# A post-norm decoder layer on one core: the next batch's first queries, keys and score maxima computed inside this batch's self attention, and cross attention scores issued for four heads at a time

## The chip, the cores and the metric

The program runs on one core of one Trainium2 chip. The metric is the device time in microseconds (us) of one execution; lower is better. TensorE is called PE here, VectorE DVE, ScalarE ACT, GpSimd POOL and SyncE SP, as the profile calls them.

## The reference

Four batches of 1024 tokens of width 256 pass through one decoder layer in float32: self attention, cross attention and a mixture of experts, each followed by a residual and a layer norm.

```python
# self attention: 16 heads of 16, scores scaled by a gate per token and head
q, k, v = heads(x @ Wq + bq), heads(x @ Wk + bk), heads(x @ Wv + bv)
scores = q @ k.T / 4 * sigmoid(x @ cg_W + cg_b + (cons_vec @ am_W + am_b))
ctx = softmax(scores) @ v
ctx = 0.3 * ctx + 0.7 * mha(x, ca)          # 4 heads of 64
ctx = (1 - META_W) * ctx + META_W * mha(ctx, mc)
x = layernorm(x + ctx @ Wo + bo)
# cross attention: 16 heads of 16, 154 keys, bias -log(distance) * |scaling|
scores = (x @ WqT + bq) / 4 @ (ctx1024 @ WkT + bk).T + bias
x = layernorm(x + softmax(scores) @ (ctx1024 @ WvT + bv) @ WoT + bo)
# top 2 of 8 experts per token, and a shared expert
x = layernorm(x + experts(x) + shared(x))
```

## The kernel before, in words

**Layout.** Token tiles have 128 partitions; `xT`, `cm` and `x1T` hold a batch transposed (features on partitions, 1024 tokens along the row). The 16 narrow heads sit four to a group of 128 partitions, each in its own 32 rows (`r = 32 * j`), so a matmul of one head uses 32 rows of PE's array. PSUM, where matmuls write, is split into a `big` ring of two tiles of two banks, a `small` ring of three tiles of one bank (`one` in the profile), and one `acc` tile.

**Self attention of a batch** (lines 944 to 979) is a loop of 128 steps. A step has two halves, for two pairs of heads that use different rows:

- `maxima(n + 12)`, lines 473 to 497: the scores of two heads, queries on partitions and 512 keys along the row (two matmuls into a `big` tile, L485), and DVE's maximum over them (L492). After every eight steps the maxima are transposed and written as one more row of the queries, so that the second scores come out with the maximum already taken off.
- `exponentials(n)`, lines 499 to 561: the scores again, keys on partitions (four matmuls of 256 columns, L518), ACT's exponential (L529), and, three steps later and once in two steps, the product with the values (L539) into a `small` tile.

The maxima run `lead = 12` steps ahead. In the last 12 steps of a batch there are none left, and `exponentials` is called with `alone=True`: its scores go into one `big` tile and one exponential of 1024 columns reads them (L526).

**Where the lead comes from.** `begin(b)` (lines 832 to 854) prepares a batch: two transposes of the tokens into `xT`; for each half of the heads a gate, the queries and the keys (`project`, three times 8 matmul instructions at L344), which go out to DRAM (`q_rows`, `k_rows`) and come back with padding rows (`load`); then 12 calls of `maxima`, each followed by one of the 8 value projections `wv` (L358), and 8 value projections for the 4-head attention. Batch 0 runs this at once. For later batches it is the generator `ahead`, advanced step by step in the batch before: twice beside the output projection (L1010 to 1014), eight times in `close_sublayer` (L1022 to 1024), and then once in each step of the cross loop.

**The rest of a batch.** Four query and key projections of the `ca` attention (`caq`) and its first two units run in the last 12 to 28 steps of self attention. Then come the `ca` and `mc` attentions (L593, L629, L647; 16 units each), the output projection, a layer norm, the keys and values of cross attention, and the cross loop (lines 1104 to 1115, 36 turns).

**The cross loop.** `scores(n)` (L717 to 752) handles two heads and two token tiles: four matmuls of 154 keys into one `big` tile (L725), then for each of the four blocks DVE adds the bias and takes the minimum (`biased`, recorded at L325) and ACT takes the exponential (L745). `flip(n - 2)` transposes (L760) into a `small` tile that ACT copies (L763), and at odd turns the last 32 keys of all four heads (L770) into another that DVE copies (L777). `product` (L786, L795) multiplies with the values into `acc`, ACT copies it (L803), and `divide` (L407 to L411) normalizes.

**What sets the order.** The source gives each engine's instructions an order; the builder's scheduler may then move a ready instruction ahead. It also assigns ring slots, so an instruction that writes a tile waits for the ring's slot to come free. The `ex` ring of SBUF tiles (10 slots, `EXB`) carries exponentials, gates, outgoing queries and keys, and transposed probabilities; the `qk` ring has 6 slots.

Of the kernel before, what the change touches and what calls it, by code (L numbers as in the profile page):

```python
# [1 line left out]

# [14 lines left out]
P = 128  # L17
# [7 lines left out]
EXB = 10  # L25
# [17 lines left out]
def run(gen):  # L43
    for _ in gen:
        pass
# [3 lines left out]
def decoder_layer(ctx: ExitStack, tc: tile.TileContext, a, out):  # L49
# [11 lines left out]
    def big():  # L61
        return pbig.tile([P, 2, 512], F32, tag="big", name="big")
# [145 lines left out]
    with tc.tile_pool(name="wA", bufs=1) as wA, tc.tile_pool(name="work", bufs=2) as work:  # L208
# [90 lines left out]
        bv = load_bcast("bv", a["L0_attn_bv"])  # L299
        for i in range(2):  # L300
            for half in range(NC2):
                nc.sync.dma_start(rows_of(i, half, HD), pads[:, i, :])

        def load_mha(k, w_out):
            win = wide.tile([P, NC2, 3 * H], F32, tag=k, name=k + "win")
            nc.sync.dma_start(win, a[f"L0_attn_{k}_Win"].rearrange("(c p) n -> p c n", p=P))
            bin_ = a[f"L0_attn_{k}_bin"]
            mbq = load_cols(k + "bq", bin_[0:H])
            mbk = load_cols(k + "bk", bin_[H : 2 * H])
            mbv = load_bcast(k + "bv", bin_[2 * H : 3 * H])  # L310
            wout = load_plain(k + "wout", a[f"L0_attn_{k}_Wout"], H)
            bout = load_cols(k + "bout", a[f"L0_attn_{k}_bout"])
            nc.vector.tensor_scalar(bout, bout, w_out, None, ALU.mult)
            return win, mbq, mbk, mbv, wout, bout
# [21 lines left out]
        def qk_tile(name):  # L336
            return work.tile([P, S], F32, tag="qk", name=name, bufs=6)
# [365 lines left out]
        class Cross:  # L703
# [13 lines left out]
            def scores(self, n):  # L717
                g, s = divmod(n, 8)
                tp, pair = divmod(s, 2)
                ps = big()  # L720
                for tt in range(2):
                    for jj in range(2):
                        r = 32 * (2 * pair + jj)
                        tok = (2 * tp + tt) * P
                        nc.tensor.matmul(  # L725
                            ps[:, jj, tt * S2 : (tt + 1) * S2],
                            self.q[g][r : r + 32, tok : tok + P],
                            self.kx[r : r + 32, g, :],
                            start=True,
                            stop=True,  # L730
                        )
                ex = ex_tile([P, 2, 2, S2], "xs")
                mx = work.tile([P, 4], F32, tag="xmx", name="xmx", bufs=3)
                for tt in range(2):
                    for jj in range(2):
                        biased(
                            ex[:, jj, tt, :],
                            ps[:, jj, tt * S2 : (tt + 1) * S2],
                            self.bias[:, 2 * tp + tt, :],
                            mx[:, 2 * tt + jj : 2 * tt + jj + 1],  # L740
                        )
                for tt in range(2):
                    for jj in range(2):
# [8 lines left out]
                self.ex[n] = ex  # L752
# [79 lines left out]
        def begin(b):  # L832

            y = ys[b]
            xT = work.tile([P, NC2, S], F32, tag="xT", name="xT", bufs=1)
            for c in range(NC2):
                transpose_tokens(xT, y, c)
                yield
            v16 = work.tile([P, NT, VP], F32, tag="v16", name="v16", bufs=1)
            nc.gpsimd.memset(v16, 1.0)  # L840
            sa = Self(xT, v16, None)
            yield from sa.project(0)
            sa.load(0)
            yield from sa.project(1)
            add_bias(y, bo)
            v64 = work.tile([P, NT, H], F32, tag="v64", name="v64", bufs=1)
            begun[b] = sa, xT, v64
            vals = values(xT, wv, 0, bv, v16, NH, HD, 1)
            for n in range(lead):
                sa.maxima(n)  # L850
                next(vals, None)
                sa.clock.step()
                yield
            yield from values(xT, ca[0], 2 * H, ca[3], v64, MH, MD, 0)
# [58 lines left out]
        run(begin(0))  # L913
# [15 lines left out]
        nds = wA.tile([P, 1], F32, tag="nds", name="nds")  # L929
        nc.sync.dma_start(nds, a["ds"].to_broadcast([P, 1]))  # L930
        nds2 = work.tile([P, 1], F32, tag="nds2", name="nds2", bufs=1)
        nc.vector.tensor_scalar(nds2, nds, -1.0, None, ALU.mult)
        nc.vector.tensor_tensor(nds, nds, nds2, ALU.min)

        behind = iter(())
        for b in range(B):
# [7 lines left out]
            sa, xT, v64 = begun[b]  # L944
# [4 lines left out]
            units = None  # L949
            for n in range(total):  # L950
# [3 lines left out]
                sa.exponentials(n, n + lead >= total)  # L954
# [55 lines left out]
            ahead = begin(b + 1) if b + 1 < B else shared_early(b - 1)  # L1010
# [85 lines left out]
            nc.vector.tensor_scalar(bf, bf, nds, None, ALU.mult)  # L1096
# [7 lines left out]
            for n in range(total + 4):  # L1104
                if n < total:
                    xa.scores(n)
                    if n % 8 == 3 and n // 8 < NG - 1:
                        xa.project_q(n // 8 + 1)
# [392 lines left out]
```

## Time and profile before

| what | us |
|---|---|
| median of 3 runs (lowest, highest) | 3205.32 (3201.66, 3207.2) |
| the profiled execution, and its span | 3203.9, 3202.1 |
| busy in the span: PE, DVE, ACT, POOL | 3100.6, 1652.9, 1613.0, 455.2 |
| batch 0 up to its first self attention step | 0 to 89.5 |
| self attention of batch 0, steps with maxima; steps without | 89.5 to about 288; to about 324 |
| `ca` and `mc` attentions | 324 to 538 |
| output projection, norm, preparation of the cross loop | 538 to 592 |
| cross loop of batch 0 | 592 to about 700 |
| first self attention steps of batches 1, 2, 3 | 702.2, 1333.5, 1965.8 |
| experts | about 2605 to 3202 |

The table's stretches are read from the timeline by the lines that run in them. Matmuls are float32 and each is recorded as two instructions, which is why L485 counts 2048 instructions for 1024 matmuls. Matmuls on different rows of the array overlap in the records, so the time that one costs is taken from the start of its group to the start of the next, not from its own duration.

### The profile page before, as it was taken

What the parts mean: (1) busy time and instruction counts of PE and PEld (TensorE: products, weight loads), DVE (VectorE), ACT (ScalarE), POOL (GpSimd) and SP (SyncE); (2) the same over time, 40 slices, a digit from 0 to 9 for tenths busy, and PEclk for the clock granted to TensorE, in tenths of its full rate; (3) what the DMA queues carried; (4) which work ended last, traced back from release to release, by engine and by line L of the source; (5) the groups of instructions that cost most, each with busy time, mean ns of one, the idle gap of its engine ahead of it and who ended that gap; (6) DMA issues with size and microseconds to landing.
All of it is one profiled execution on the core that took longest, in us unless ns stands there. A gap on an engine that the chain in (4) does not pass through costs nothing.

```text
span 3202.1 us, 61771 instructions
## 1 busy us (share of the span) xinstructions
PE 3100.6 (97%) x25602; PEld 1956.8 (61%) x25602; DVE 1652.9 (52%) x3459; ACT 1613.0 (50%) x3235; POOL 455.2 (14%) x757
## 2 busy tenths in 40 slices
PE   7999999999999999999999999999999999899995
PEld 3665766566657665666576666665666665566663
DVE  3774655567746555677465565774555551111112
ACT  1676534466756344667554346766453631233333
POOL 1111001001110000011100100110000016333331
PEclk7999999999999999999999999999999999999997
DMA  7300000101000001100000100000000052222224
GB/s 222 101 2 1 1 1 2 49 29 41 2 1 1 1 17 37 38 28 2 1 1 1 34 23 23 15 2 11 1 11 1 5 203 104 66 45 47 47 45 125
DMA packets 83325, 111.04 MB, mean 35 GB/s; under 512 B 8832, under 2 KB 69224, under 8 KB 83048
## 3 DMA queue, kind: packets, MB, share of 16 engines
q1 hardware_dynamic: 69752, 89.33, 9.0%
q0 software_dynamic: 13296, 17.77, 3.3%
q8 instruction: 204, 3.34, 0.4%
q14 instruction: 73, 0.60, 0.1%
HBM read 58.97 MB, written 48.11 MB: 33 GB/s over the span
## 4 chain that ended last, share of the span: by engine, by line
PE 89%; DMA 4%; ACT 2%; DVE 2%; issue 1%; POOL 1%; SPq 0%; ACTq 0%; POOLq 0%; DVEq 0%
PE big L485 9%; PE one L539 8%; PE big L593 8%; PE one L629 8%; PE big L1334 8%; PE big L344 8%; PE acc L647 8%; PE one L518 7%; PE acc L1360 4%; PE one L358 3%; PE big L725 3%; PE one L760 2%; PE big L693 2%; DMA scratch<-y,where 1%; PE big L518 1%
## 5 line engine op out<-in xcount | busy, mean ns | idle before, releaser
L492 DVE TENSOR_REDUCE mxp<-big 128x2 f32<-128x1024 f32 x512 | 611.4, 1220 | 239.2 <-PE one L518 169.2
L485 PE MATMUL big<-k,q 31*128 31x512 f32 x2048 | 562.0, 630 | 9.7 <-DMA k<-k_rows 3.7
L529 ACT ACTIVATE ex<-one 128x512 f32<-128x512 f32 x696 | 372.9, 597 | 255.3 <-PE one L518 189.1
L518 PE MATMUL one<-q,k 32*128 32x256 f32 x2784 | 479.1, 397 | 0.0
L325 DVE CUSTOM_DVE_ANT_0 prob<-big,zero_t 128x1024 f32<-128x1024 f32 x256 | 303.8, 1222 | 272.3 <-PE big L593 272.1
L518 PEld LDWEIGHTS one<-q,k 32*128 32x128 f32 x2784 | 322.1, 185 | 27.7 <-DVE q L402 9.2
L612 ACT ACTIVATE prob<-prob,nmx 128x1024 f32<-128x1024 f32 x256 | 293.0, 1152 | 18.6 <-DVE nmx L325 18.5
L634 ACT COPY pt<-one 128x512 f32<-128x512 f32 x256 | 137.7, 590 | 302.7 <-PE one L629 302.7
L539 PE MATMUL one<-ex,v 128*32 128x256 f32 x4096 | 278.4, 390 | 1.5
L593 PE MATMUL big<-mk,mq 64*128 64x512 f32 x1024 | 278.4, 616 | 0.0
L629 PEld LDWEIGHTS one<-ident,prob 128*128 128x128 f32 x2048 | 219.0, 140 | 96.3 <-issue 90.1
L485 PEld LDWEIGHTS big<-k,q 31*128 31x128 f32 x2048 | 195.2, 188 | 129.2 <-issue 102.4
L1334 PE MATMUL big<-wall,xt 128*128 x568 | 268.3, 596 | 1.9 <-issue 1.9
L555 POOL TENSOR_TENSOR avq<-avq,avp 128x256 f32<-128x256 f32 x192 | 139.2, 725 | 887.4 <-ACT avp L554 887.4
L629 PE MATMUL one<-ident,prob 128*128 128x128 f32 x2048 | 255.2, 277 | 0.1
L518 PE MATMUL acc<-q,k 32*128 32x256 f32 x928 | 247.3, 385 | 0.0
L1344 DVE TENSOR_TENSOR hidr<-big,slr 128x512 f32<-128x512 f32 x71 | 49.1, 691 | 373.5 <-ACT slr L1342 373.5
L745 ACT ACTIVATE xs<-xs,xmx 128x154 f32<-128x154 f32 x512 | 175.2, 412 | 109.7 <-DVE xmx L325 109.7
L539 PEld LDWEIGHTS one<-ex,v 128*32 128x32 f32 x4096 | 107.7, 110 | 147.6 <-ACT ex L529 80.6
L636 DVE COPY pt<-one 128x512 f32<-128x512 f32 x256 | 164.3, 683 | 9.1 <-PE one L629 9.1
L518 PEld LDWEIGHTS acc<-q,k 32*128 32x128 f32 x928 | 163.8, 184 | 0.0
L325 DVE CUSTOM_DVE_ANT_0 xs<-big,bias 128x154 f32<-128x154 f32 x512 | 132.6, 313 | 53.4 <-PE big L725 45.6
(270 smaller groups left out, 4590.3 us busy)
## 6 DMA issues: line engine op xcount, KB each, us to landing
scratch<-empty SPq DMA_DIRECT2D x1, 9159.0 KB
xg<-scratch SPq DMA_DIRECT2D x71, 129.0 KB
q<-q_rows SPq DMA_DIRECT2D x16, 512.0 KB
k<-k_rows SPq DMA_DIRECT2D x16, 512.0 KB
y<-in_x_dram SPq DMA_DIRECT2D x4, 1024.0 KB
q_rows<-qh SPq DMA_DIRECT2D x8, 512.0 KB
k_rows<-kh SPq DMA_DIRECT2D x8, 512.0 KB
wall<-in_L_ffn_w_gate_dram SPq DMA_DIRECT2D x8, 512.0 KB
```

Of the source, the lines that this page charges most:

```text
L325: nc.vector.tensor_tensor_reduce(out=out, in0=ps, in1=bias, scale=-1.0, scalar=3.0e38, op0=ALU.add, op1=ALU.min, accum_out=low,)
L344: nc.tensor.matmul(ps[:, tb, :], w[:, c, lo : lo + P], xT[:, c, tb * 512 : (tb + 1) * 512], start=(c == 0), stop=(c == NC2 - 1),)
L485: nc.tensor.matmul(ps[:, jj, :], st["q"][r : r + MR, tok : tok + P], st["k"][r : r + MR, kb * 512 : (kb + 1) * 512], start=True, stop=True,)
L492: nc.vector.reduce_max(mxp[:, t, kb, 2 * pair : 2 * pair + 2], ps, axis=AX.X)
L518: nc.tensor.matmul(scs[jj][:, i * QW : (i + 1) * QW], st["k"][r : r + MR + 1, kc * P : (kc + 1) * P], st["q"][r : r + MR + 1, part * QW : ...
L529: nc.scalar.activation(ex[:, jj, :], scs[jj], AF.Exp, scale=1.0 / HD**0.5)
L539: nc.tensor.matmul(av[32 * j : 32 * j + 32, 0:QW], self.v[:, kc, h * VW : h * VW + 32], exs[kcp, j // 2][:, j % 2, i * QW : (i + 1) * QW], ...
L593: nc.tensor.matmul(pss[i][:, kb, :], q[r : r + MD, t * P : (t + 1) * P], k[r : r + MD, kb * 512 : (kb + 1) * 512], start=True, stop=True,)
L612: nc.scalar.activation(p, p, AF.Exp, bias=nmx[:, i : i + 1], scale=-1.0, accum_out=sm[:, t % 4, i : i + 1],)
L629: nc.tensor.transpose(ps[:, kc * P : (kc + 1) * P], probs[u][i][:, at : at + P], ident)
L647: nc.tensor.matmul(av[64 * i : 64 * i + 64, (t % 4) * P : (t % 4 + 1) * P], v[:, kc, h * MD : (h + 1) * MD], flipped[u][i][:, kc, :], star ...
L1334: nc.tensor.matmul(ps[:, g, :], xt[:, c * P : (c + 1) * P], wall[:, bass.ds(off + (g * NC2 + c) * D, D)], start=(c == 0), stop=(c == NC2 - 1),
```

## The change

Nothing is computed differently; work changes its place and its grouping.

- `begin` is split. `early(b + 1)` makes the transposed tokens (in the `cm` slot), the first half's gate, queries and keys, and loads them back; it is advanced at every eighth step from step 66 of batch b's self attention. `late(b + 1)` transposes the same tokens again into `xT` and does the second half, all values, and nothing else; it takes the place of `begin` as `ahead`.
- The 12 leading maxima of batch b + 1 are called in the last 12 steps of batch b's self attention; those steps no longer run `alone` (except in the last batch).
- In batch 0, the first 6 of the 16 value projections come ahead of the 12 maxima, the other 10 between them.
- `Cross.scores` is called at even turns only and handles all four heads: eight matmuls into two `big` tiles, in the order of the heads' rows, then the eight bias additions and eight exponentials.
- `EXB` goes from 10 to 9 and the `qk` ring from 6 to 8 slots. Three scalings go from DVE to POOL (`bout` of `ca` and `mc`, and the bias by `nds`); `nds` is loaded at the start.

```diff
-EXB = 10
+EXB = 9
...
+        nds = wA.tile([P, 1], F32, tag="nds", name="nds")
+        nc.sync.dma_start(nds, a["ds"].to_broadcast([P, 1]))
...
-            return work.tile([P, S], F32, tag="qk", name=name, bufs=6)
+            return work.tile([P, S], F32, tag="qk", name=name, bufs=8)
...
             def scores(self, n):
                 g, s = divmod(n, 8)
-                tp, pair = divmod(s, 2)
-                ps = big()
+                tp = s // 2
+                pss = [big(), big()]
                 for tt in range(2):
-                    for jj in range(2):
-                        r = 32 * (2 * pair + jj)
+                    for j in range(4):
+                        r = 32 * j
                         tok = (2 * tp + tt) * P
                         nc.tensor.matmul(
-                            ps[:, jj, tt * S2 : (tt + 1) * S2],
+                            pss[j // 2][:, j % 2, tt * S2 : (tt + 1) * S2],
...
+                for pair, ps in enumerate(pss):
+                    ex = self.ex[n + pair] = ex_tile([P, 2, 2, S2], "xs")
+                    mx = work.tile([P, 4], F32, tag="xmx", name="xmx", bufs=3)
...
-        def begin(b):
+        def early(b):
+            xT = work.tile([P, NC2, S], F32, tag="xT" if b == 0 else "cm", name="xT", bufs=1)
             for c in range(NC2):
-                transpose_tokens(xT, y, c)
+                transpose_tokens(xT, ys[b], c)
                 yield
+            sa = Self(xT, None, None)
+            begun[b] = sa
             yield from sa.project(0)
             sa.load(0)
+
+        def late(b):
+            sa = begun[b]
+            if b > 0:
+                sa.xT = work.tile([P, NC2, S], F32, tag="xT", name="xT", bufs=1)
+                for c in range(NC2):
+                    transpose_tokens(sa.xT, ys[b], c)
+                    yield
+            xT = sa.xT
             yield from sa.project(1)
...
+            if b == 0:
+                for _ in range(6):
+                    next(vals)
+                for n in range(lead):
+                    sa.maxima(n)
+                    next(vals, None)
+                    sa.clock.step()
+            yield from vals
...
+            soon = early(b + 1) if b + 1 < B else iter(())
             for n in range(total):
                 g, s = divmod(n, 32)
                 if n + lead < total:
                     sa.maxima(n + lead)
-                sa.exponentials(n, n + lead >= total)
+                elif b + 1 < B:
+                    after = begun[b + 1]
+                    after.maxima(n + lead - total)
+                    after.clock.step()
+                sa.exponentials(n, n + lead >= total and b + 1 == B)
+                if n >= 64 and n % 8 == 2:
+                    next(soon, None)
...
-            ahead = begin(b + 1) if b + 1 < B else shared_early(b - 1)
+            ahead = late(b + 1) if b + 1 < B else shared_early(b - 1)
...
-            nc.vector.tensor_scalar(bf, bf, nds, None, ALU.mult)
+            nc.gpsimd.tensor_scalar(bf, bf, nds, None, ALU.mult)
...
-                if n < total:
+                if n < total and n % 2 == 0:
                     xa.scores(n)
```

More of the change, by code (lines that the diff above doesn't have):

```diff
@@ L1 @@
 from contextlib import ExitStack
+from itertools import chain
 import concourse.bass as bass
@@ L299, in decoder_layer @@
         bv = load_bcast("bv", a["L0_attn_bv"])
+        nds = wA.tile([P, 1], F32, tag="nds", name="nds")
+        nc.sync.dma_start(nds, a["ds"].to_broadcast([P, 1]))
+        nds2 = work.tile([P, 1], F32, tag="nds2", name="nds2", bufs=1)
+        nc.vector.tensor_scalar(nds2, nds, -1.0, None, ALU.mult)
+        nc.vector.tensor_tensor(nds, nds, nds2, ALU.min)
         for i in range(2):
@@ L312, in load_mha @@
             bout = load_cols(k + "bout", a[f"L0_attn_{k}_bout"])
-            nc.vector.tensor_scalar(bout, bout, w_out, None, ALU.mult)
+            nc.gpsimd.tensor_scalar(bout, bout, w_out, None, ALU.mult)
             return win, mbq, mbk, mbv, wout, bout
@@ L731, in scores @@
                         )
[L732 to L735, printed above, removed]
+                for pair, ps in enumerate(pss):
+                    ex = self.ex[n + pair] = ex_tile([P, 2, 2, S2], "xs")
+                    mx = work.tile([P, 4], F32, tag="xmx", name="xmx", bufs=3)
+                    blocks = [(tt, jj) for tt in range(2) for jj in range(2)]
+                    for tt, jj in blocks:
+                        i = 2 * tt + jj
                         biased(
@@ L739, in scores @@
                             self.bias[:, 2 * tp + tt, :],
-                            mx[:, 2 * tt + jj : 2 * tt + jj + 1],
+                            mx[:, i : i + 1],
                         )
-                for tt in range(2):
-                    for jj in range(2):
+                    for tt, jj in blocks:
                         i = 2 * tt + jj
@@ L751, in scores @@
                         )
-                self.ex[n] = ex
             def flip(self, n):
@@ L830, in decoder_layer @@
         begun = {}
-        def begin(b):
-            y = ys[b]
-            xT = work.tile([P, NC2, S], F32, tag="xT", name="xT", bufs=1)
+        def early(b):
+            xT = work.tile([P, NC2, S], F32, tag="xT" if b == 0 else "cm", name="xT", bufs=1)
             for c in range(NC2):
-                transpose_tokens(xT, y, c)
+                transpose_tokens(xT, ys[b], c)
                 yield
-            v16 = work.tile([P, NT, VP], F32, tag="v16", name="v16", bufs=1)
-            nc.gpsimd.memset(v16, 1.0)
-            sa = Self(xT, v16, None)
+            sa = Self(xT, None, None)
+            begun[b] = sa
             yield from sa.project(0)
             sa.load(0)
-            yield from sa.project(1)
[L845 to L854, printed above, removed]
+        def late(b):
[6 more added lines that the diff above has]
+            xT = sa.xT
+            yield from sa.project(1)
+            add_bias(ys[b], bo)
+            sa.v = v16 = work.tile([P, NT, VP], F32, tag="v16", name="v16", bufs=1)
+            nc.gpsimd.memset(v16, 1.0)
+            sa.v64 = v64 = work.tile([P, NT, H], F32, tag="v64", name="v64", bufs=1)
+            vals = chain(
+                values(xT, wv, 0, bv, v16, NH, HD, 1),
+                values(xT, ca[0], 2 * H, ca[3], v64, MH, MD, 0),
+            )
+            if b == 0:
[6 more added lines that the diff above has]
+            yield from vals
         def end(b, cx4):
@@ L911, in shared_early @@
             return shared(ys[b], room, gated, add, True)
-        run(begin(0))
+        run(early(0))
+        run(late(0))
         load_y(1)
@@ L927, in decoder_layer @@
         xbo = load_bcast("xbo", a["L0_xattn_bo"])
[L929 to L933, printed above, removed]
         behind = iter(())
@@ L942, in decoder_layer @@
             nc.sync.dma_start(cn, a["ctx_1024"][b].rearrange("(c p) d -> p c d", p=HK))
-            sa, xT, v64 = begun[b]
+            sa = begun[b]
+            xT, v64 = sa.xT, sa.v64
             sa.ctok = ctok = work.tile([P, NT, H], F32, tag="ctok", name="ctok", bufs=1)
@@ L1104, in decoder_layer @@
             for n in range(total + 4):
-                if n < total:
+                if n < total and n % 2 == 0:
                     xa.scores(n)
-                    if n % 8 == 3 and n // 8 < NG - 1:
-                        xa.project_q(n // 8 + 1)
+                if n < total and n % 8 == 3 and n // 8 < NG - 1:
+                    xa.project_q(n // 8 + 1)
                 if 2 <= n < total + 2:
```

## The prediction

> **What bounds the kernel.** I read the page's first two sections first, then the stretches by stage, then PE's timeline inside each stage that the change touches.
>
> ```profile
> PE 3100.6 (97%) x25602; PEld 1956.8 (61%) x25602; DVE 1652.9 (52%) x3459; ACT 1613.0 (50%) x3235; POOL 455.2 (14%) x757
> ...
> PEclk7999999999999999999999999999999999999997
> ```
>
> PE is busy for 97% of the span, every other engine for about half. Time is won or lost as PE's time, in one of three forms: work taken from it, work of several heads that overlaps on different rows of its array, and clock. The clock's two low slices are the first and the last. The stretches, with columns PE, weight loads, DVE, ACT, POOL and the granted clock, show the first:
>
> ```profile
> 43.00:90.00 47.00, 45.28 (x118) 21.96 (x122) 22.63 (x34) 2.60 (x2) 1.49 (x4) 0.60 0.85 250
> 90.00:288.00 198.00, 196.26 (x2365) 121.22 (x2357) 149.96 (x159) 138.67 (x288) 30.47 (x42) 1.00 0.10 28
> 288.00:324.00 36.00, 35.58 (x280) 18.49 (x280) 8.41 (x15) 21.92 (x33) 5.71 (x7) 1.00 0.00 1
> 592.00:700.00 108.00, 106.63 (x1050) 62.87 (x1050) 69.48 (x334) 66.05 (x178) 0.51 (x2) 1.00 0.09 27
> ```
>
> Row one is batch 0's maxima and values: clock 0.60. Row three is the last steps of self attention, without maxima: PE full, DVE busy for 8.41 of 36 us. Row four is the cross loop: PE full. PE's timeline shows what overlaps (start, length, group):
>
> ```profile
> 604.70 1.13 PE L485 MATMUL big<-k,q 31*128 31x512 f32 x4
> 605.76 1.13 PE L358 MATMUL one<-wv,xT 128*128 128x256 f32 x4
> ...
> 666.45 0.79 PE L725 MATMUL big<-kx,xq 32*128 32x154 f32 x8
> 667.18 0.65 PE L760 MATMUL one<-ident,xs 128*122 128x128 f32 x4
> ...
> 669.33 0.79 PE L725 MATMUL big<-kx,xq 32*128 32x154 f32 x8
> ...
> 748.28 1.07 PE L539 MATMUL one<-ex,v 128*32 128x256 f32 x16
> ...
> 751.21 1.07 PE L539 MATMUL one<-ex,v 128*32 128x256 f32 x16
> ```
>
> A call of maxima in the cross loop holds PE from 604.70 to 605.76, 1.06 us. In self attention two whole steps, maxima included, and one product go from 748.28 to 751.21: 2.93 us, less about 1.00 for the product is 0.97 a step. A step without maxima goes from 308.40 to 309.46, 1.06 us. So maxima beside exponentials are free, and beside anything else cost 1.06.
>
> **The change, part by part**, against the profiled execution: span 3202.1, time 3203.9 (1.4 under the median, 3205.32).
>
> *Maxima moved.* At 576 to 632, 1207 to 1264 and 1838 to 1895 PE runs 48 instructions of L485 each, which is 12 calls, and from start to next start they take 12.0 us. Three times that leaves: -36. In their new place a step goes from 1.06 to 0.97 by those rows; by the mean over 97 steps of batch 1 (101 us of L485 and L518 starts) it is 1.04. I take 0, with +3 as the bound. DVE gets 12 x 1.22 = 14.7 us more on 8.41 of 36, ACT two exponentials of 0.60 for one of 1.02; both stay far under PE. What waits there is the `big` ring: a maximum needs one of two tiles, and at steps 24 and 28 a unit of the `ca` attention takes both until DVE has read them (2 x 1.22). Behind a waiting matmul everything on PE queues. Two such waits of up to 1.5 us a batch bound it at +9; with the tenth `ex` slot gone as well I take +4.
>
> *Early part.* Projections only move. Added are two transposes of the tokens a batch: 8 instructions and 1.04 us each, 3 x 2.08 = +6. Three projections and two transposes in the middle of the steps break into the ring like `caq` does today, where 2 of 4 projections have 0.45 us of idle PE ahead of them: five times 0.2 in three batches, +3. Their ACT copies (2 x 1.01) and evictions (1.1 each) fit, since ACT has 59 of 198 us free there and DVE 48. The tanh costs no table load: at 1199.39 it runs and exponentials follow at 1224.32 without one. The DRAM round trip took 12 us (keys evicted at 1195, loaded at 1207); the source now leaves 10 steps, some 15 us, behind the load: nothing. In the norm after self attention the chain from the last output matmul (1195.92) to the normed tokens (1200.93) is 5.0 us. It used to have 20 us of PE work over it, and keeps five values and the cross preparation, 5.3 + 4.4: still covered.
>
> *Cross scores.* One call of two heads takes 0.72 us from start to next start (666.45 to 667.18), 32 calls 22.9 us a batch. In it the four passes of a head follow each other at 0.13, after 0.24 of filling and before 0.22 of draining. Four heads run in the same passes: 73.33 starts four of L485 within 0.02 us of each other. Within a pass the matmuls start 0.007 apart, so the eight further instructions add at most 0.05 and a call of four heads takes 0.77: 16 x (1.43 - 0.77) x 4 batches = -42. A turn of two then needs 4.41 - 0.66 = 3.75 us of PE where nothing else is mixed in. Now ACT is there too. Its exponentials follow each other at 0.313:
>
> ```profile
> 675.05 1.36 ACT L745 ACTIVATE xs<-xs,xmx 128x154 f32<-128x154 f32 x4 [0.57 <-DVE xmx L325]
> 676.32 0.56 ACT L763 COPY xpt<-one 122x512 f32<-122x512 f32 x1
> ```
>
> Eight of them 2.50, two copies 0.47 each, one of 0.33: 3.77 a turn of two, as much as PE. DVE needs 8 x 0.238 + 0.35 + 0.45 = 2.7. And the copies stand behind eight exponentials instead of four. Written out in source order, with scores from 0: DVE from 0.82, ACT from 1.18 to 3.69, copy to 4.15. The three `small` tiles are then taken by two flips and a `divide`; the tile of L770 comes free when DVE has done the divide (3.2), then L770 and the product, next scores at 4.8. The scheduler may put the product ahead of L770, which gives 3.9. Of 16 turns about half carry values or a query projection, which keep PE full; for the other half I take 4.15, between 3.77 and 4.8 and nearer to the full engines. That gives back 8 x 0.4 x 4 = +13. Net -29, from -42 to +25 (all 64 turns at 4.8).
>
> The Trainium skill has a rule against this part (TensorEngine Tiling (Array Packing), PSUM Bottleneck): tiled matmuls get faster but their eviction does not, which may become the bound. The rows above agree as far as that ACT, at 3.77, comes level with PE.
>
> *Batch 0.* PE idles from 39.22 to 42.89 for keys from DRAM; then the clock is low, and a call of maxima and a value go at 2.08 each instead of 1.06:
>
> ```profile
> 42.89 1.26 PE L485 MATMUL big<-k,q 31*128 31x512 f32 x4 [3.67 <-DMA k<-k_rows]
> ...
> 45.23 2.08 PE L485 MATMUL big<-k,q 31*128 31x512 f32 x4
> 47.24 2.08 PE L358 MATMUL one<-wv,xT 128*128 128x256 f32 x4
> ```
>
> Low clock lasts from 43.75 to 84.71 but for 3.4 us, and the first self step starts at 89.54. With six values in front PE has 6.4 us of work from 39.22, and the keys are there at 42.89. If the clock stays up as it does for the same mix at 1207 to 1211, ten pairs of 2.12 follow (66.8), then two maxima at DVE's pace (1.22 each) and the tail: about 70. That is -19.5; at half clock throughout the maxima it is +1.5.
>
> The Trainium skill (TensorE: Matmul & The Clock Gate, Part 1) says that an idle window of about 3.4 us drops the clock and that as much sustained work releases it. The trace agrees with the first half (3.67 us of idle, then 0.5), by which closing the gap is enough and the sum takes -19.5. It disagrees with the second: PE is counted busy for 31.00 of 31.00 us from 43 to 74 at a clock of 0.51. So busy time alone doesn't hold the clock, and the other end, +1.5, keeps a chance (rival 3).
>
> *Small things.* The bias scaling leaves DVE (0.85) for POOL, whose row of 1024 columns (the gate at 1200.59) takes 1.24 and which is idle then; `nds` adds one SP issue of 0.43 to a queue that has ended up waiting for the keys' eviction anyway. 0, at most 0.5 either way.
>
> **Sum:** -36 + 4 + 6 + 3 - 29 - 19.5 = -71.5, so 3203.9 - 71.5 = 3132.
>
> **The rivals.**
>
> 1. *Slower: the cross loop locks step.* One call takes both `big` tiles, and L770 waits for the copy that stands behind eight exponentials: 4.25 + 0.46 + 1.1 = 5.9 us a turn instead of 4.41. Then +95 replaces the -29: 3256. It decides against the change above 5.07, where it eats up the other 42.5 us (0.66 x 64). Against it: instructions move ahead in this program. Maxima of the next batch run at 691.95 between two flips of the cross loop, though the source has them behind it. For it: DVE and ACT already wait on each other there (0.57 in the row above). 0.08.
> 2. *The cross loop wins nothing*, 4.4 to 4.8 a turn: 3161 to 3186. The same if four heads didn't overlap in PSUM. 0.16.
> 3. *The clock stays low in batch 0*, since maxima fill half of the array's rows, and the clock dropped again at 77.88 in a stretch of them: +1.5 for -19.5, 3153. 0.13.
> 4. *Everything fits*, no waits in the ring and ACT hidden: 3132 - 13 - 7 = 3112 and a few below. 0.15.
>
> The forecast as summed, 3115 to 3148, has 0.45. A remaining 0.03 goes to a balance within 0.2% (6.4 us, about what a measurement of this kernel can tell from no change). Faster: 0.45 + 0.16 + 0.13 + 0.15 = 0.89; same 0.03; slower 0.08. The range of 8 in 10 takes in cases 2 to 4: 3100 to 3184.
>
> **What would show it.** After: no L485 groups of their own outside self attention except in batch 0; L526 only in the last batch; the first self step of batch 1 about 34 us earlier than 702.2 (19.5 + 36/3 + 29/4 - 13/3); L725 groups of x16 of about 0.8 us, some 3.75 to 4.2 apart late in the loop; PE busy some 70 us less at nearly the same share; clock near 1 from 20 to 90. Idle PE ahead of L760, L770 or L725, released by ACT, would prove rival 1 or 2. I would be wrong altogether if PE idled in the last 12 steps for `big` or `ex` slots.

## The result, and the profile after

| | before | after |
|---|---|---|
| median, us (runs, lowest to highest) | 3204.8 (4, 3201.66 to 3207.2) | 3160.77 (4, 3157.03 to 3162.9) |
| profiled execution; its span | 3203.9; 3202.1 | 3162.9; 3161.1 |
| first self step of batch 0 | 89.5 | 67.1 |
| first self steps of batches 1, 2, 3 | 702.2, 1333.5, 1965.8 | 676.9, 1302.4, 1924.4 |

The ratio is 0.9852 (0.9839 to 0.9865): 1.5% faster, by 41.0 us in the profiled executions, where the sum had 71.5. After is inside the predicted range and 30 us above the sum's 3132. Line numbers have grown, by 7 up to the middle of the program and by more behind it: L485, L518, L593, L725, L760, L770 are now L492, L525, L600, L733, L768, L778.

The page of the changed kernel:

```profile
PE 3061.7 (97%) x25650; PEld 1932.4 (61%) x25650; DVE 1648.6 (52%) x3453; ACT 1617.5 (51%) x3277; POOL 466.9 (15%) x763
...
PEclk9999999999999999999999999999999999899997
```

PE still bounds, at the same 97%; its busy time fell by 38.9 us. The low first slice of the clock is gone, but a slice late in the run now shows 8. The stretches of the changed kernel (PE, weight loads, DVE, ACT, POOL, granted clock):

```profile
43.00:66.90 23.90, 22.86 (x91) 10.49 (x90) 17.47 (x24) 0.00 (x0) 1.70 (x5) 1.00 0.71 203
67.10:265.00 197.90, 196.46 (x2238) 118.33 (x2242) 141.38 (x148) 135.75 (x273) 32.69 (x41) 1.00 0.26 74
265.00:301.00 36.00, 35.28 (x328) 18.48 (x321) 23.05 (x27) 20.14 (x40) 3.62 (x5) 1.00 0.00 1
578.70:676.90 98.20, 95.74 (x1010) 57.75 (x1010) 54.33 (x319) 68.08 (x182) 3.79 (x3) 0.93 0.10 29
```

Row one, batch 0's maxima and values, went from clock 0.60 to 1.00. Row three holds the next batch's maxima: DVE does 23 us of work where it did 8. Row four is the cross loop: shorter than the 108 us of before, but its clock is 0.93 instead of 1.00. That is the first trace of what went missing.

Where the time went, by the starts of the stages in both traces:

| stage, all four batches | predicted | measured |
|---|---|---|
| start to batch 0's first self step | -19.5 | -22.4 |
| self attention (+57.8; +20.8, +18.8, +18.5, -0.3) with the preparation of the cross loop (-33.8) | -32.4 + 32.4 + 9 + 4 = +13 | +24.0 |
| cross loops (-12.2, -13.4, -17.9, -1.5) | -36 - 29 = -65 | -45.0 |
| the rest | 0 | +2.4 |

The 32.4 are the three early projections of a batch, 10.8 us in each of three batches, which change their stage. The missing 30 us lie in two rows: 11 in self attention, 20 in the cross loops.

### The profile page after: what moved, and what is told of

Its sections match the earlier page's. It is cut to its first block, busy times and chain, and to the rows that moved or that the text cites. A ratio compares the mean times of both kernels' runs of the same rounds, so it can differ in the third digit from the quotient of the medians.

```text
span 3161.1 us, 62092 instructions
## 1 busy us (share of the span) xinstructions
PE 3061.7 (97%) x25650; PEld 1932.4 (61%) x25650; DVE 1648.6 (52%) x3453; ACT 1617.5 (51%) x3277; POOL 466.9 (15%) x763
## 4 chain that ended last, share of the span: by engine, by line
PE 90%; DMA 4%; DVE 3%; ACT 1%; issue 1%; POOL 1%; SPq 0%; ACTq 0%; POOLq 0%; DVEq 0%
PE big L492 9%; PE one L546 8%; PE big L351 8%; PE one L525 8%; PE big L600 8%; PE big L1361 8%; PE one L636 8%; PE acc L654 8%; PE acc L1387 4%; PE one L365 2%; PE big L733 2%; PE one L768 2%; PE big L700 2%; DMA scratch<-y,where 2%; PE acc L803 1%; PE big L194 1%
## 5 line engine op out<-in xcount | busy, mean ns | idle before, releaser
L492 PE MATMUL big<-k,q 31*128 31x512 f32 x2048 | 567.1, 623 | 4.0 <-DVE mxp L499 4.0
L536 ACT ACTIVATE ex<-one 128x512 f32<-128x512 f32 x750 | 405.3, 597 | 269.6 <-PE one L525 180.3
L525 PE MATMUL one<-q,k 32*128 32x256 f32 x3000 | 527.1, 399 | 0.2
L525 PEld LDWEIGHTS one<-q,k 32*128 32x128 f32 x3000 | 346.9, 185 | 38.0 <-DVE q L409 13.2
L619 ACT ACTIVATE prob<-prob,nmx 128x1024 f32<-128x1024 f32 x256 | 293.0, 1152 | 18.8 <-DVE nmx L332 18.8
L600 PE MATMUL big<-mk,mq 64*128 64x512 f32 x1024 | 277.7, 617 | 1.5 <-DVE mxp L499 1.5
L492 PEld LDWEIGHTS big<-k,q 31*128 31x128 f32 x2048 | 197.0, 185 | 127.7 <-issue 109.1
L525 PE MATMUL acc<-q,k 32*128 32x256 f32 x1000 | 270.8, 389 | 0.0
L754 ACT ACTIVATE xs<-xs,xmx 128x154 f32<-128x154 f32 x512 | 167.2, 410 | 47.5 <-DVE xmx L332 46.7
L525 PEld LDWEIGHTS acc<-q,k 32*128 32x128 f32 x1000 | 175.3, 185 | 0.1
L600 PEld LDWEIGHTS big<-mk,mq 64*128 64x128 f32 x1024 | 95.9, 186 | 98.4 <-issue 77.7
```

The source lines that it names most:

```text
L492: nc.tensor.matmul(ps[:, jj, :], st["q"][r : r + MR, tok : tok + P], st["k"][r : r + MR, kb * 512 : (kb + 1) * 512], start=True, stop=True,)
L525: nc.tensor.matmul(scs[jj][:, i * QW : (i + 1) * QW], st["k"][r : r + MR + 1, kc * P : (kc + 1) * P], st["q"][r : r + MR + 1, part * QW : ...
L536: nc.scalar.activation(ex[:, jj, :], scs[jj], AF.Exp, scale=1.0 / HD**0.5)
L600: nc.tensor.matmul(pss[i][:, kb, :], q[r : r + MD, t * P : (t + 1) * P], k[r : r + MD, kb * 512 : (kb + 1) * 512], start=True, stop=True,)
L619: nc.scalar.activation(p, p, AF.Exp, bias=nmx[:, i : i + 1], scale=-1.0, accum_out=sm[:, t % 4, i : i + 1],)
```

## The experiments

Ratios are to the kernel before, with 95% intervals; 0.001 is 3.2 us. The kernel before was measured again beside each group of runs (medians 3209.1, 3208.1 and 3208.3), so a median here doesn't compare with the 3204.8 above, only its ratio does. The length of a cross loop is taken from its first scores to the next batch's first self step, in the last batch to its last product. "Low clock" is the time at half speed, by the trace's clock record, within the loops of batches 0 to 2; it is 3.4 us before and 27.1 us after. Where PE is busy throughout, a loop loses half of it.

### One part at a time

The kernel before, with the grouped scores and their loop only.

```diff
+                pss = [big(), big()]
...
-                if n < total:
+                if n < total and n % 2 == 0:
                     xa.scores(n)
```

> The kernel before with the cross scores of four heads together as the only edit (ring sizes as before). Theory 1 (PE's time decides, and the grouping saves what the changed kernel's L733 groups show against L725, 22.9 to about 16.5 us a batch): 22 to 27 us under the kernel before, some 3179, with the clock staying up at both ends of the cross loop, since the maxima are still mixed into it. Rival (the cross loop is held by ACT and the two big tiles, so grouping wins nothing): within 5 us of before.

Measured: 3202.33, 0.998 (0.9969 to 0.9992), or 6.4 us instead of 29. The scores themselves go from 22.9 to 16.7 us in each of the first three batches, but the loops take 112.1, 108.9, 110.6 and 93.9 us instead of 110.2, 110.4, 111.8 and 96.7. PE idles 3 us more in each of the first three: 1.7 us of it ahead of scores, until DVE has read a maximum (the maxima of the next batch and the scores of four heads want the same two `big` tiles), the rest mostly behind ACT. Low clock is 10.2 us, 6.8 of it in the first loop. With half of the low clock taken off, the first three loops win 1.2 to 1.5 us each, and the last, which holds no maxima, 4.5.

The early part and the moved maxima only: the changed kernel with the ungrouped scores, DVE's scalings and the old order of batch 0's values.

```diff
-                for _ in range(6):
-                    next(vals)
                 for n in range(lead):
                     sa.maxima(n)
-                    next(vals, None)
+                    if n < NT:
+                        next(vals, None)
```

> Early queries and keys and the 12 maxima moved into the last steps of self attention, with the ring sizes that this needs; cross scores, batch 0's order and the scalings as before. Theory 1 (36 us of maxima leave the cross loop, some 17 come back in self attention because a step with maxima costs 1.08 and not 0.97 and waits for big tiles, 9 for the second transposes and waits of the projections): 10 us under the kernel before if the clock holds, near 0 if the emptied ends of the cross loop drop it. Rival (moved maxima are free, as I had predicted, and the loss is elsewhere): 23 us under.

Measured: 3206.41, 0.9975 (0.9959 to 0.9991), 8 us. Self attention grows by 19.2, 20.4 and 26.7 us, the preparations shrink by 11 each, the cross loops only by 10.9, 8.9 and 11.8 where 12 us of maxima left each. Low clock is 24.6 us, and a stretch at half clock from 1320.8 to 1341.3 runs on into the self attention that grows by 26.7. Theory 1 gave 10 us with the clock held and near 0 without; the rival's 23 us fall.

The early values of batch 0 only.

```diff
+            rest = values(xT, ca[0], 2 * H, ca[3], v64, MH, MD, 0)
+            if b == 0:
+                vals = chain(vals, rest)
+                for _ in range(6):
+                    next(vals)
```

> The kernel before with batch 0's values ahead of and between the maxima as the only edit. Theory 1 (the clock stays up in batch 0): 20 to 23 us under the kernel before, and no low clock between 20 and 90 us. Rival (the changed kernel's clear start comes from its other edits): under 5 us.

Measured: 3206.78, 0.9994 (0.9982 to 1.0007): nothing, with the first self step at 89.4. DVE's timeline shows why:

```profile
46.03 0.41 DVE L367 TENSOR_TENSOR v<-one,bv 128x256 f32<-128x256 f32 x1
56.49 0.17 DVE L314 TENSOR_SCALAR mcbout<-mcbout 128x2 f32<-128x2 f32 x1 [10.04 <-DMA mcbout<-in_L_attn_mc_bout_dram]
```

And PE's timeline of the same run:

```profile
49.01 1.13 PE L359 MATMUL one<-cawin,xT 128*128 128x256 f32 x4
57.84 2.08 PE L486 MATMUL big<-k,q 31*128 31x512 f32 x4 [7.70 <-DVE mxp L493]
```

A scaling of two columns, 0.17 us long, stands at the head of DVE's queue until `mcbout` has been loaded. The values are evicted by DVE, so they and the maxima wait behind it; PE runs out of tiles, idles for 7.70 us and comes back at half clock (2.08 us for 1.06). The gap that the early values close has only changed its place.

The small things only: `EXB`, `qk`, the scalings on POOL, `nds` at the start.

```diff
-EXB = 10
+EXB = 9
...
-            nc.vector.tensor_scalar(bout, bout, w_out, None, ALU.mult)
+            nc.gpsimd.tensor_scalar(bout, bout, w_out, None, ALU.mult)
...
-            nc.vector.tensor_scalar(bf, bf, nds, None, ALU.mult)
+            nc.gpsimd.tensor_scalar(bf, bf, nds, None, ALU.mult)
```

> The kernel before with the ring sizes (9 and 8) and the moved scalings and early load of nds alone. Theory 1: within 3 us of before. Rival (one ex slot less makes waits in the steps or in the 4-head attentions): 5 to 15 us slower.

Measured: 3205.46, 0.9986 (0.9975 to 0.9997), 4.5 us; the first self step comes at 86.3, 3.2 us earlier, so most of it may lie ahead of that.

The four ratios fall short of 1 by 0.0065 together, give or take 0.0026, though the second and the fourth share the ring sizes and the early `nds`; the whole change falls short by 0.0148. About half of it appears only when parts stand together.

### Batch 0: which waits hold it

The early values with `bout` scaled on POOL.

```diff
-            nc.vector.tensor_scalar(bout, bout, w_out, None, ALU.mult)
+            nc.gpsimd.tensor_scalar(bout, bout, w_out, None, ALU.mult)
```

> The kernel before with the early values of batch 0 and with the scaling of bout on POOL in place of DVE, nothing else. The early values alone gained nothing: DVE stood at that scaling from 46.4 to 56.5 us, waiting for the load of mc's bout, PE waited with it for 7.7 us and the clock was low from 53.5 on. Theory 1 (the scaling's wait in DVE's queue is what cost the clock): 19 to 23 us under before, 0.993 to 0.994, with no low clock from 20 to 90 us. Rival (the wait for nds, still on DVE, does the same a little later): under 5 us.

Measured: 3203.58, 0.9985 (0.9974 to 0.9996). The wait is followed by the next one in the queue, as DVE's waits between 20 and 90 us show (us in total, times, longest):

```profile
DVE qh L457 <- PE big L345: 20.2, 2, 11.2
DVE nds L938 <- DMA nds<-in_ds_dram: 10.9, 1, 10.9
```

`nds`, wanted much later by the source, is computed from a load that stands late in the DMA queue; PE has a gap of 8.78 us behind it, and the first self step comes at 82.7.

With that one gone too:

```diff
+        nds = wA.tile([P, 1], F32, tag="nds", name="nds")
+        nc.sync.dma_start(nds, a["ds"].to_broadcast([P, 1]))
...
-            nc.vector.tensor_scalar(bf, bf, nds, None, ALU.mult)
+            nc.gpsimd.tensor_scalar(bf, bf, nds, None, ALU.mult)
```

> The kernel before with four edits that belong to batch 0 and its prologue: the early values, the scaling of bout on GpSimd, the scaling of the bias on GpSimd, and nds loaded at the top of the program. The values alone and with bout gave -2 and -4.5 us: VectorE stood 10.04 us at a scaling whose load was late, then 10.94 us at the next one (nds). My theory: with both taken from VectorE's queue, no wait of over 2 us is left ahead of the first self step, it comes at about 67 us instead of 89.5, the granted clock does not fall between 20 and 90 us, and the kernel is 20 to 23 us faster, 0.993 to 0.994 of before. Rival: a third wait or the DMA queue itself takes their place (the values then come ahead of the loads that they need), the first step stays at 80 us or later, and under 8 us are won, 0.9975 or more.

Measured: 3190.86 (3180.99 to 3206.53, 12 runs), 0.9951 (0.9934 to 0.9968), 16 us. DVE's waits between 39 and 66.5 us are now of another kind, for PE's own results:

```profile
DVE mxp L499 <- PE big L492: 6.3, 11, 0.9
DVE v L373 <- PE one L365: 3.0, 3, 1.3
```

The first self step comes at 66.5, 23 us earlier, as the theory had it, and the rival falls. Two signs that the theory named didn't come: PE still waits once 2.9 us (from 35.1, for an eviction of values), and the clock falls for 3.4 us at 39.2 and at 73.3. Only 12.6 us of the 23 reach the end of the profiled execution, and 16 the median ratio: self attention of batch 0 takes 4.6 us longer (among others, PE waits 1.57 us for an exponential at 70.1, and 3.4 us run at half clock), and the cross loops 7 together, in two of which the clock falls for 6.8 us. Nor does every execution win: nine of the twelve take 3181 to 3193 us at a mean granted clock of 0.986 to 0.989, the other three 3200 to 3207 at 0.980 to 0.982, where the runs of the kernel before have 0.977 to 0.984. The size is thus below what the theory gave.

### Self attention: the shared `big` tiles

The first two `ca` units only after the last self steps, except in the last batch.

```diff
-                if g == 3 and s in (24, 28):
+                if g == 3 and s in (24, 28) and b == B - 1:
```

> The changed kernel with the first two units of the ca attention after the steps and not inside the last 12 (batches 0 to 2). Theory 1 (in these steps a unit and the moved maxima wait for each other's big tiles, 1.4 us at each of two units a batch): the scores groups of units 0 and 1 (L600) take 2.0 us again and not 3.3, and 5 to 9 us are gained, 0.9825 to 0.984. Rival (the units were the work that covered ACT's and DVE's tails of the steps, and the waits only move behind the loop): 0 to 8 us slower.

PE's timeline of the changed kernel shows one of the two units:

```profile
293.98 0.70 PE L525 MATMUL one<-q,k 32*128 32x256 f32 x4
...
295.05 1.12 PE L600 MATMUL big<-mk,mq 64*128 64x512 f32 x2
296.42 1.98 PE L600 MATMUL big<-mk,mq 64*128 64x512 f32 x6 [0.26 <-DVE mxp L499]
298.33 0.48 PE L525 MATMUL one<-q,k 32*128 32x256 f32 x1
```

A unit of `ca` scores goes from 295.05 to 298.33, 3.28 us, and the next one likewise (305.90 to 309.19). The first quarter fills one tile, the rest waits for DVE to read a maximum out of the other. That these two units take longer is not new, though. In the kernel before they took 3.42 and 3.17 us:

```profile
299.55 3.17 PE L593 MATMUL big<-mk,mq 64*128 64x512 f32 x8
302.97 1.13 PE L518 MATMUL big<-q,k 32*128 32x256 f32 x8 [0.25 <-DVE nmx L325]
...
309.46 3.23 PE L593 MATMUL big<-mk,mq 64*128 64x512 f32 x8
312.63 1.99 PE L629 MATMUL one<-ident,prob 128*128 128x128 f32 x16
```

Measured with the edit: 3151.55, 0.9821 (0.9808 to 0.9834), 10 us better than the change. Self attention shrinks by 4.1, 3.5 and 3.6 us in batches 0 to 2; low clock is 33.9. The units do not go back to 2.0 us as the theory said: the first two take 3.96 and 2.83, and the first three together 8.7 instead of 10.5. The other 2 us a batch are won in the steps. From the first score matmul of the 117th step to the last of the 128th, without the units and transposes between them, batch 1 takes 16.7 us before, 20.6 in the changed kernel and 18.7 here. So of the 4 us that these steps lost by the change, the units beside them cost half; the other half stays without them. The 1.8 us won on the units themselves were no part of what was missing, since before the units took as long.

### The cross loop: clock, division, grouping

Low clock went from 3.4 to 27.1 us. Stretches of the changed kernel at the two ends of the first cross loop:

```profile
578.20:581.60 3.40, 1.97 (x26) 1.14 (x24) 3.17 (x20) 1.69 (x3) 0.00 (x0) 1.00 0.01 2
581.60:588.40 6.80, 6.73 (x20) 4.25 (x21) 2.33 (x17) 5.19 (x17) 0.00 (x0) 0.50 0.01 2
666.90:670.30 3.40, 2.49 (x24) 0.80 (x20) 1.72 (x3) 2.19 (x3) 1.35 (x1) 1.00 0.00 0
670.30:677.10 6.80, 6.80 (x30) 4.37 (x23) 0.50 (x2) 2.22 (x5) 2.43 (x3) 0.50 0.00 0
```

In 3.4 us PE is busy for 1.97, then for 2.49 us, and each time the next 6.8 us run at 0.50. At the end of the loop the last chain (transposes, ACT's copies, products) has nothing beside it; before, the maxima lay there. At its start PE idles for 1.13 us, and ACT loads a table at the first exponential:

```profile
579.90 1.28 ACT L754 ACT_TABLE_LOAD   x1 [5.51 <-DVE xmx L332]
581.20 1.05 ACT L754 ACTIVATE xs<-xs,xmx 128x154 f32<-128x154 f32 x3
```

Next, the next batch's values kept for the ends of the loop: taken in its first and last turns, and only four of the eight steps beside the norm.

```diff
-                if b < B - 1 or n % 2 == 0:
+                if n < 4 if b < B - 1 else n % 2 == 0:
                     next(ahead, None)
...
-                if b < B - 1 or n in (6, 12, 18, 24):
+                if n in (6, 12, 18, 24) if b == B - 1 else n < 8 or n > 28:
                     next(ahead, None)
```

> The changed kernel with the 15 last values of the next batch kept for both ends of the cross loop (turns 0 to 7 and 29 to 35) and not for the norm and the turns 0 to 10. Theory 1 (PE has nothing to put beside the first and last turns since the maxima are gone, its clock drops there for 3.4 to 6.8 us, and the values cure both): no low clock within the cross loops of batches 0 to 2 and 10 to 17 us under the changed kernel, ratio 0.980 to 0.982. Rival (the drops are there whatever is mixed in, or what is saved is lost in the norm, whose chain of 5.0 us then has 4.4 us of cover): 0 to 4 us slower, 0.985 to 0.987.

Measured: 3151.93, 0.9828 (0.9814 to 0.9843), 8 us better than the change. Low clock is 17.1 us. Stretches of this run:

```profile
579.30:582.70 3.40, 3.40 (x12) 2.36 (x9) 1.46 (x9) 3.40 (x13) 0.00 (x0) 0.50 0.00 0
...
664.00:671.00 7.00, 7.00 (x58) 4.98 (x57) 2.47 (x8) 3.26 (x6) 3.12 (x3) 1.00 0.00 0
```

The fall at the end of batch 0's loop is cured: PE is full and the clock at 1.00; so is the one at the end of batch 1's (1295.0 in the changed kernel). The one at the start is still there (579.3, 1197.1 and 1818.3), so the theory holds for one end. The table load isn't needed for it: in the changed kernel's last batch ACT loads its table 16 us ahead of the loop, and the clock falls all the same, 2.8 us into it and for 6.8 us. In the 9 us from 1 us ahead of their first scores PE idles 1.5 us in the changed kernel's first three loops and 1.8 in the last; in the first three of before, which keep their clock, it idles 0.5. But the last loop of before idles 1.9 us there and keeps its clock too, so idle time alone doesn't settle it.

Then the division of the turns. PE's timeline of the changed kernel, late in the loop:

```profile
643.70 0.65 PE L768 MATMUL one<-ident,xs 128*122 128x128 f32 x4
...
646.07 0.53 PE L733 MATMUL big<-kx,xq 32*128 32x154 f32 x4
646.53 0.65 PE L778 MATMUL one<-ident,xs 128*32 128x128 f32 x16
647.10 0.79 PE L733 MATMUL big<-kx,xq 32*128 32x154 f32 x12
647.83 0.65 PE L768 MATMUL one<-ident,xs 128*122 128x128 f32 x4
```

The sixteen instructions (eight matmuls, each recorded as two) run as 4, then the last keys of the pair before, then 12: 0.46 + 0.73 us instead of 0.77. A turn of two goes from 643.70 to 647.83, 4.13 us. The first attempt ordered the last keys of a pair behind the scores of the next pair:

```diff
+                with tc.issue_after(self.last.ins):
+                    for tt in range(2):
+                        for j in range(4):
+                            nc.tensor.matmul(
+                                ps[32 * j : 32 * j + 32, tt * P : (tt + 1) * P],
```

> The changed kernel with one order forced: the tail transposes of the last 32 keys (L778) may not be issued on PE between two parts of a scores call. In the changed kernel they stand there in about 40 of 64 turns, and a turn takes 4.13 us, with scores of 0.46 + 0.73 in place of 0.77. Theory 1 (the split costs, up to the pace of ACT, whose work of a turn lies some 3.95 apart): 7 to 10 us under the changed kernel, ratio to before 0.982 to 0.984. Rival A (PE's order alone decides): 18 us under, 0.9797. Rival B (the two big tiles are not free any earlier, so PE now waits where it was split): no change, 0.985 to 0.987.

Measured: 3165.42, 0.9867 (0.985 to 0.9883). The edit missed: the division stays in the trace as 4 and 12, because the last keys that come between belong one pair earlier than those that it orders. It tells nothing about the division, but it is in effect the changed kernel measured once more: 0.9867 beside 0.9852. Against this repeat, which was measured beside them, the units after the steps win 15 us and the values at the ends 12, not 10 and 8.

Then both repairs together, the values at the ends and the units after the steps:

> Both repairs together: the value steps of the next batch at the two ends of the cross loop, and the first units of mha issued only after the last self steps. Each alone won 9 us against the changed kernel (3151.9 and 3151.6). They sit in stages far apart, the one at the cross loop's ends and after it, the other before the output projections. My theory: they add, 3141 to 3144 us, 0.9795 to 0.981 of before. Rival: both remove the same loss, a low clock that one of them cures as well, and together give no more than one, 0.982 to 0.983.

Measured: 3136.04, 0.9781 (0.9763 to 0.9798), 23 us better than the change where the single ones gave 8 and 10 (28 against the repeat, for 12 and 15). They add; this is the fastest version run. Low clock is 17.1 us.

On top of these, the scores issued behind the last keys that did come between:

```diff
+                with tc.issue_after(self.tail.ins) if self.tail else ExitStack():
+                    for tt in range(2):
+                        for j in range(4):
...
-                        nc.tensor.matmul(
+                        self.tail = nc.tensor.matmul(
                             ps[32 * j : 32 * j + 32, tt * P : (tt + 1) * P],
```

> Both repairs, and each group of sixteen... of eight cross score matmuls (32 rows x 154, two big tiles) issued only behind the last tail matmul of the pair before, so that TensorE does them as one piece; in the changed kernel late turns run them as 4, then the tail, then 12. My theory: the division is what holds a turn at 4.13 us; in one piece, scores are 12 to 13 us a batch instead of 16 to 17.5, a turn goes at ScalarE's pace of 3.9 to 4.0 us, and four batches win 6 to 9 us against the run with both repairs alone. Rival: TensorE now waits at the head of the scores for the tail's exponentials, so that a turn stays at 4.1 us or more and nothing is won, within 3 us of the run with both repairs or slower.

Measured: 3142.13, 0.9811 (0.9788 to 0.9835), no better than without. Now the scores are one piece and take 13.1 to 13.4 us in each of the first three batches instead of 17.2 to 17.3, yet a turn still takes 4.10 us. PE's timeline of this run:

```profile
637.14 0.64 PE L780 MATMUL one<-ident,xs 128*32 128x128 f32 x16 [0.35 <-DVE xtok L418]
637.71 0.81 PE L735 MATMUL big<-kx,xq 32*128 32x154 f32 x16
...
641.24 0.64 PE L780 MATMUL one<-ident,xs 128*32 128x128 f32 x16 [0.35 <-DVE xtok L418]
```

And DVE's in that turn:

```profile
638.66 0.32 DVE L332 CUSTOM_DVE_ANT_0 xs<-big,bias 128x154 f32<-128x154 f32 x1 [0.40 <-PE big L735]
...
640.57 0.20 DVE L417 RECIPROCAL rs<-one 128x8 f32<-128x8 f32 x1
640.80 0.29 DVE L418 TENSOR_TENSOR xtok<-one,rs 128x128 f32<-128x128 f32 x1
```

The records form a ring: PE's last keys at 637.14 and scores to 638.5, DVE's eight bias additions from 638.66, behind them in its queue the division, which ends at 641.09, and with it a `small` tile comes free for the next last keys at 641.24. So the division of the turn was no loss in these turns; PE filled with it a time in which it would wait. A shorter ring would win little, since ACT is busy for 3.83 of the 4.10 us. The rival holds, with another releaser than it named (DVE's division, not ACT's exponentials). The prediction's place in the Trainium skill (TensorEngine Tiling (Array Packing), PSUM Bottleneck: faster tiled matmuls leave the eviction as the bound) agrees with this run: 4 us less of scores a batch, and a turn that doesn't move.

Last, the changed kernel with the scores of two heads again:

```diff
-                pss = [big(), big()]
+                ps = big()
...
-                if n < total and n % 2 == 0:
+                if n < total:
                     xa.scores(n)
```

> The changed kernel with the cross scores of two heads at a time again; the rest of the change is kept. My theory: by itself the grouping won 7 us, since the maxima and the scores of that loop both draw on the big tiles; with the maxima gone the tiles are free, and the grouping is worth its full 6 to 7 us a batch, so without it the cross loops take about 105 to 107 us each instead of 95 to 99 and the kernel is 20 to 26 us behind the changed one, 0.992 to 0.9935 of before. Rival: the grouping is worth no more here than alone, since its turns are divided on TensorE (4.13 us instead of 4.41): 6 to 8 us, 0.9865 to 0.988 of before.

Measured: 3184.11, 0.9928 (0.991 to 0.9946). Grouping is worth 24 us in the changed kernel (0.9928 - 0.9852; 20 against the repeat), three to four times what it is worth alone. The theory's size holds, its picture of the loops only in part: they take 97.5, 102.5, 97.6 and 98.3 us, not 105 to 107 each, where the changed kernel's take 98.3, 97.0, 93.6 and 95.3. With half of the low clock taken off, grouping wins 4.2, 3.9, 4.0 and 4.7 us, 17 in all; alone it won that much only in the last loop, the one without maxima. Of the rest, some lies in one stretch of 20.5 us at half clock at the end of batch 1's loop, which runs on into self attention.

```profile
1301.00:1321.50 20.50, 20.50 (x69) 12.36 (x68) 3.79 (x10) 6.21 (x10) 3.37 (x3) 0.50 0.00 1
```

In its loops the low clock is 20.3 us, less than in the changed kernel, so grouping gained nothing through the clock.

## Why the prediction was right in direction and 30 us off

**Batch 0: right, for a reason that the sum had at nothing.** -22.4 for -19.5, clock 1.00, maxima and values in pairs of 2.12 as worked out. But the "small things" carry it: without the scalings on POOL and the early `nds`, the same values gave nothing (89.4, 82.7, then 66.5 for the first self step). I had looked at what DVE does, not at what it waits for once PE no longer stands still at 39 us. Rival 3 (clock stays low) fell.

**Maxima moved: the wrong step.** "I take 0" for the steps themselves, and "two such waits of up to 1.5 us a batch bound it at +9; ... I take +4". The last 12 steps of a batch, from the first score matmul to the last, take 29.2 us where they took 25.2, so three batches lost 12 us where the sum had 4; that is the two bounds, +3 and +9, together. Of the 11 us missing in self attention these are 8; the others are small (2 us more around the moved projections, 1.7 in batch 0's first steps). The mechanism was the one named for half of it, 2 us a batch, which come back when the units leave these steps. The other half, 2 us a batch, is what the maxima cost there without them, and no run shows why.

**What left the cross loop also left its clock.** The "-36" is right as PE time, but it counted the maxima as work only. They were what PE did while the loop filled and drained. Low clock rose by 24 us in the first three loops and by 7 in the last, 15 us of loss at half speed. Refilling the ends with values took 10 us of low clock away, worth 5 of the 8 us that this won. No term of the sum held this. The loops bear it out: with half of the low clock taken off, the first three take 110.1 to 110.4 us before and 91.6 to 91.9 after, a gain of 18.4 where the sum had 19.25 (12 of maxima, 7.25 of scores). So 15 of the 20 us missing in the cross loops are clock. The traces agree with each other: low clock is 3.4 to 10.2 us in the six where the maxima stay, 20.3 to 33.9 in the five where they go, and 10.2 to 17.1 in the three where values replace them. I named the clock only in batch 0. And "the tanh costs no table load" is right for where the gate went, but not for what it left: before, ACT loaded the table for the gate 25 us ahead of the loop; now the loop's first exponential loads it.

**Cross scores: -24 for -29.** The loops themselves hold 17 of the 24. The source-order estimate of 4.15 us a turn met 4.13, but for all late turns, and, by the run with the scores in one piece, from a ring over DVE's division rather than ACT's copies; so that the number met is partly luck. Rival 1 (whose 5.9 us adds up to 5.8) fell. Rival 2 (nothing won) is nearly true of the grouping alone, 6 us, and false in the changed kernel: with the maxima gone it had the `big` tiles to itself. That the measured time lies outside the forecast as summed (3115 to 3148) and at the lower end of rival 2's times (3161 to 3186) is chance: the clock and the moved maxima took it there. Rival 4 fell with the turn of 4.13.

**Sum.** By the runs: batch 0 about -16, early part and maxima about -7 (0.9951 to 0.9928), grouping -24, in all -47 of the median ratio; predicted -19.5, -23 and -29. Each of these differences has an interval of 5 to 8 us. Two thirds of the shortfall is the middle term. The early part itself was right: transposes 2.1 us of work a batch, projections 10.9. Of the named checks, the first self step of batch 1 came 25.3 us earlier instead of 34, PE's busy time fell by 38.9 instead of 70; and PE waited for `big` in the last 12 steps, the sign named for being wrong, though the loss was 4 us a batch and not the whole gain.

What stays open: what lets the clock fall at the start of the cross loop, and what the moved maxima wait for in their steps once the units are gone.

## What to carry to other kernels

Work that is moved away from a stage's ends is also the cover of its filling and draining: before moving it, ask what PE does in those few us, and leave something small there. A tiny instruction that waits for a DMA at the head of an in-order queue can hold up a whole prologue, and taking one such wait away shows the next; list all of them before pricing. Two edits that draw on the same ring of tiles can't be priced one by one: here the parts alone gave 0.0065 and together 0.0148.

## What the runs showed of the hardware

- The clock fell after stretches in which PE was busy for 1.97 and 2.49 of 3.4 us, with no single idle time over 1.13 us, though another with 2.41 of 3.4 (before, 696.00 to 699.40) left it at 1.00; and it stayed at 0.50 for 20.50 us in which PE was busy for 20.50. The Trainium skill (TensorE: Matmul & The Clock Gate, Part 1) lets it fall after an idle window of about 3.4 us and rise after as much sustained work; the multiples of 3.4 us are in the records, but in these stretches neither condition is.
- The bias scaling, 128 x 1232 elements, took 3.40 us on POOL (four times, all within 0.03 us), where DVE took 0.85 and the estimate from the gate's row was 1.24. It lay off the path.
